# A token's place in the expert lists: two products over 24 and 16 columns in place of five over eight

## The chip, the cores and the metric

The kernel runs on one core of a Trainium2 chip. The core has four engines that compute and that run side by side, each with its own queue in order: TensorE (PE in the profile; its weight loads have a row of their own, PEld), VectorE (DVE), ScalarE (ACT) and GpSimd (POOL). SyncE (SP) issues transfers. The metric is the device time of one execution in microseconds (us), as the median of several runs.

## The reference

The inputs are `x` (4 x 512 tokens of 256), a context `ctx_1024` (4 x 1024 x 256), a mask and weights. The computation has two parts.

1. Cross attention with 16 heads of 16: `x = x + attention(layernorm(x), ctx, mask)`.
2. A block over the batch (the four entries of the first axis attend to each other, 16 query heads and 4 key heads), and then a mixture of experts: layer norm, a router over 8 experts, the two best experts for each token, for each of them `gelu(x w1) w2`, weighted by the router's probabilities:

```python
logits = einsum('th,eh->te', x, router_weight)
top_probs, top_idx = top_k(softmax(logits), 2)
h_mid = gelu(einsum('th,ehf->etf', x, moe_w1))
expert_out = einsum('etf,efh->eth', h_mid, moe_w2)
```

All is in float32.

## The kernel before

**Experts by lists.** A token's row is computed only by its two experts. For that, each expert has a list in a table in DRAM (2048 places for each expert), and each token's row is scattered to its place in two lists. Later the lists are read back in tiles of 128 rows, and each tile goes through one expert (`expert_x`, `expert_up`, `expert_down`). There are 39 such tiles. They are taken in lists that become known one after another: "a" (9 tiles), "b" (8), and "c" with "d" (22), whose places are only known when the last tokens have been routed.

**A half.** The second block works on halves: batch b and 256 of its 512 tokens, two tiles of 128, so there are eight halves (b, h). The generator `half(b, h)` holds the work of one in some 21 pieces, and each `yield` ends a piece. Behind the router (psl) it computes the softmax, the best expert and the second best, as zeros and ones over 8 experts in `picks[:, 0]` and `picks[:, 1]` (128 tokens in partitions x 2 tiles x 8). `chosen` is their sum: two tiles of 128 x 8 with a one where a token goes to that expert.

**The place.** A token's place in an expert's list is the list's length so far (`base`), plus the number of tokens before it in its own tile that go to that expert, plus, for the second tile, all of the first tile. TensorE counts that: with `before`, a 128 x 128 triangle of ones, and `ones`, 128 x 128 of ones. In the bank `psr` columns 0:8 get `before` x first tile, columns 8:16 get `before` x second tile + `ones` x first tile, and columns 16:24 get `ones` x both tiles, which is what is added to `base`. These are five products (L622 to L627). VectorE reads them (`place` L630, the new `base` L636), multiplies by `picks`, sums (`pos` L641) and makes whole numbers (`index` L643). GpSimd scatters the rows by `index` with four indirect DMAs (L653).

**What orders the work.** The order on every engine is written out by the program (`manual_schedule`): an engine takes its instructions as the Python code emits them.

- In the attention stage the code goes through 139 steps (10 of them ahead). A step has the maxima products (psm L1147, four), the score products (pss L1168, four), the exponentials on ScalarE, the maxima on VectorE (mx L1154), and the products with the values (av L1186). Other work is put behind a step by a planner, `Plan`: each piece has a cost on TensorE, a cost on VectorE, and a first and a last step. `spread` puts pieces into steps in order of their last step, by a rate, and with at most 2.0 of VectorE's cost in a step where a piece may still wait; `level` then moves pieces to where a step's modelled length grows least. The costs of the pieces of a half stand in `PARTS` as (TensorE, lag in steps, VectorE). The piece that picks the second expert has (0, 1, 1.6), the piece with the five products (1.1, 1, 1). Halves (0,0), (0,1), (1,0), (1,1) and the larger part of (2,0) and some of (2,1) are placed so.
- In the expert stage the code emits tile after tile and keeps a modelled clock for each engine (`clock`, `passed`). The rest of the halves (2,1), (3,0) and (3,1) is emitted between the tiles' pieces when the modelled clock of TensorE reaches the time due. The strings of the `yield`s are these costs: `"P1.1 D1"` says that the piece takes 1.1 on TensorE and then 1 on VectorE.

The pool `k2` gives each name two buffers, so `chosen` has two.

Of the kernel before, what the change touches and what calls it, by code (L numbers as in the profile page):

```python
# [7 lines left out]
F32 = mybir.dt.float32  # L8
I32 = mybir.dt.int32
AF = mybir.ActivationFunctionType  # L10
ALU = mybir.AluOpType
# [4 lines left out]
P = 128  # L16
B, S, SK, D = 4, 512, 1024, 256
H, DK, KVH, REP = 16, 16, 4, 4
E, F = 8, 512
# [154 lines left out]
def kernel(  # L174
# [21 lines left out]
    nc = tc.nc  # L196
# [3 lines left out]
    k2 = ctx.enter_context(tc.tile_pool(name="k2", bufs=2))  # L200
# [7 lines left out]
    def bank(name, maxima=False):  # L208
        if ahead[0] and not maxima:
            return pss.tile([P, 512], F32, tag="s", name=name)  # L210
        return psw.tile([P, 512], F32, tag="w", name=name)
# [202 lines left out]
    def half(b, h):  # L414


        n = f"{b}_{h}"
# [27 lines left out]
        for i in range(2):  # L445
            ps = bank(f"psq{n}_{i}")
            for c in range(KC):
# [4 lines left out]
                    start=(c == 0),  # L452
                    stop=(c == KC - 1),
# [85 lines left out]
        for i in range(2):  # L539
            ps = bank(f"psp{n}_{i}")  # L540
            for c in range(KC):
# [4 lines left out]
                    start=(c == 0),  # L546
                    stop=(c == KC - 1),
# [23 lines left out]
        ps = bank(f"psl{n}")  # L571
        for i in range(2):
            for c in range(KC):
# [4 lines left out]
                    start=(c == 0),  # L578
                    stop=(c == KC - 1),
                )  # L580
        small = [P, 2, E]
# [17 lines left out]
        def largest(dst, src, k):  # L599

            g = gate[:, b, t0 : t0 + 2, k : k + 1]
            nc.vector.tensor_reduce(gate[:, b, t0 : t0 + 2, k], src, AX.X, ALU.max)
            nc.vector.tensor_tensor(cand, src, g.to_broadcast(small), ALU.is_equal)
            nc.vector.tensor_tensor(cand, cand, ranks, ALU.mult)
            nc.vector.tensor_reduce(m, cand, AX.X, ALU.max)
            nc.vector.tensor_tensor(dst, cand, m.to_broadcast(small), ALU.is_equal)
# [2 lines left out]
        yield "D1.7"  # L609
        nc.vector.scalar_tensor_tensor(left, picks[:, 0], -2.0, lg, ALU.mult, ALU.add)  # L610
        largest(picks[:, 1], left, 1)
        chosen = k2.tile(small, F32, tag="chosen", name=f"chosen{n}")
        nc.vector.tensor_tensor(chosen, picks[:, 0], picks[:, 1], ALU.add)
        nc.gpsimd.tensor_copy(rows[:, :, D : D + E], picks[:, 0])
        token = named["token"]
        nc.gpsimd.tensor_copy(rows[:, :, D + E], token[:, NQT * b + t0 : NQT * b + t0 + 2])
# [2 lines left out]

        base, before, ones = named["base"], named["before"], named["ones"]  # L620
        ps = bank(f"psr{n}")
        nc.tensor.matmul(ps[:, 0:E], before, chosen[:, 0, :], start=True, stop=True)  # L622
        nc.tensor.matmul(ps[:, E : 2 * E], before, chosen[:, 1, :], start=True, stop=False)
        nc.tensor.matmul(ps[:, E : 2 * E], ones, chosen[:, 0, :], start=False, stop=True)
        for i in range(2):
            nc.tensor.matmul(
                ps[:, 2 * E : 3 * E], ones, chosen[:, i, :], start=(i == 0), stop=(i == 1)  # L627
            )
        place = k2.tile(small, F32, tag="place", name=f"place{n}")
        nc.vector.tensor_tensor(  # L630
            place,
# [9 lines left out]
        nc.vector.tensor_reduce(pos, picks, AX.X, ALU.add)  # L641
        index = k2.tile([P, 2, 2], I32, tag="index", name=f"index{n}")
        nc.vector.tensor_copy(index, pos)  # L643
        yield "P1.1 D1"
        for i in range(2):
            for k in range(2):
                scatter(index[:, k, i : i + 1], rows[:, i, :], scattered, "rows")
# [4 lines left out]
    def scatter(index, rows, group, name):  # L652
# [13 lines left out]
    PARTS = [  # L666
        (0, 1, 1.7), (0, 2, 1.9), (0.45, 1, 0), (1.3, 1, 0.4), (1.3, 1, 0.4), (0, 1, 0), (0, 2, 1.8),
        (0, 1, 0.8), (0, 1, 0), (0.45, 2, 0), (0.86, 1, 0.5), (0.86, 1, 0.5), (0, 1, 1.4),
        (0, 2, 1.3), (0.45, 1, 0), (0.9, 1, 0.4), (0, 1, 1.7), (0, 1, 1.6), (1.1, 1, 1), (0, 1, 0),
        (0, 1, 0),  # L670
    ]

# [212 lines left out]
    def project_o(b, t):  # L885
# [9 lines left out]
        nc.vector.tensor_tensor(xt[:, b, t, :], ps[:, 0:D], xt[:, b, t, :], ALU.add)  # L895

    halves = {(b, h): half(b, h) for b in range(B) for h in range(2)}

    with ExitStack() as actx:
# [67 lines left out]
        ps = bank("psmask")  # L967
# [8 lines left out]
        ps = bank("psfac")  # L976
# [242 lines left out]
        for b in range(B):  # L1219
            first = 32 * b - 32  # L1220
            if b:
                turned, projected = [], []
                for kc in range(NKC):
                    p = plan.add(
                        0.86,
                        first + (6 if kc > 3 else 1),
                        first + 4 + 11 * kc // 5,
                        project_k,
                        b,
                        kc,  # L1230
                        behind=projected[-1] if kc else None,
                        also=turned[kc - KRING] if kc >= KRING else None,
# [17 lines left out]
                for h in range(2):  # L1250
                    p = plan.add(0, first + 1, first + 3 + 3 * h, statistics_x, b, h, vector=1.4)
                    p = plan.add(
                        0,
                        first + 4,
                        first + 10 + 3 * h,
                        normalize_x,
                        b,
                        h,
                        behind=p,
                        lag=2,  # L1260
# [11 lines left out]
            for kc in range(NKC):  # L1272
                start = 32 * b - 10 + kc if kc >= 4 else kc if b == 1 else 32 * b - 34 + kc
                start = max(start, START + 1)
# [10 lines left out]
            p = divided[b * NC + NC - 1]  # L1285
            q = p
            for t in range(NQT):
                p = plan.add(
                    0.86, 32 * b + 34, 32 * b + 38 + t // 2, project_o, b, t, behind=q, vector=0.4
                )  # L1290
            for h in range(2):
                start = 32 * b + (40 if b < 2 else 38) + 4 * h
# [7 lines left out]
                p = None  # L1300
# [20 lines left out]
        p = lists_due  # L1321
        for n in range(3):
            p = plan.add(0, START, END - 10, next, first_list, None, behind=p, vector=1.8)
        p = plan.add(0, 8 * M - 8, END - 2, load_list, "a", FIRST, rows_a, behind=p)
# [51 lines left out]
        for T in range(START, END):  # L1376
            ahead[0] = T < 0
            n, kc = divmod(T, 8)
# [47 lines left out]
    start = late["start"] = epool.tile([P, 2 * E], F32, name="start")  # L1426
# [176 lines left out]
    n = 0  # L1603
    while going or n < len(tiles) + 2:
        if n < len(tiles) or not going:
            for behind, piece, args, work in PIECES:
# [5 lines left out]
                name, i = tiles[k][0:2]  # L1612
# [101 lines left out]
```

## Time and profile before

| | |
|---|---|
| median of 3 runs | 836.48 us (836.19 to 838.76) |
| profiled execution: its own time | 840.55 us |
| its span, first to last instruction | 838.8 us |
| TensorE busy | 791.9 us (94%) |
| VectorE busy | 561.7 us (67%) |
| ScalarE busy | 441.9 us (53%) |
| GpSimd busy | 290.0 us (35%) |
| mean granted TensorE clock | 0.985 |

The last score product of the attention stage ends at 634.1 us, the last product with the values at 637.3 us; the expert stage fills the rest. The five products run eight times:

| half | VectorE's `chosen` (L613) at | first product (L622) at |
|---|---|---|
| (0,0) | 351.57 | 354.97 |
| (0,1) | 372.20 | 373.84 |
| (1,0) | 526.49 | 529.04 |
| (1,1) | 544.89 | 550.20 |
| (2,0) | 630.83 | 631.72 |
| (2,1) | 643.85 | 647.20 |
| (3,0) | 712.32 | 714.37 |
| (3,1) | 722.07 | 723.72 |

A float32 product has two records for its two passes, so the five products of a half are ten records on TensorE and ten weight loads. A row of a timeline gives the start, the length from the first to the last of its records, the engine, the line, the operation, what is written and read, the shape and the number of records; in brackets stands the idle time of the engine before it and what ended it.

### The profile page before, as it was taken

Reading aid. Unit: us, or ns where it says so; the run is one execution under the profiler, and the core shown is the slowest. Engines: PE = TensorE matmul, PEld = TensorE weight load, DVE = VectorE, ACT = ScalarE, POOL = GpSimd, SP = SyncE. Lnnn points to the kernel's source line nnn. Section 1 sums busy time; section 2 is a strip of 40 time slices with the busy share of each in tenths; the row PEclk is TensorE's granted clock in tenths of the full one; section 3 lists DMA queues with packets and bytes.
Section 4 is the critical chain, followed back from the end, with each engine's and each line's share of the span. In section 5 each row is a group of like instructions: output and inputs, shape, how many; then the busy total and the mean of one; then the engine's idle time right before and its main releaser. Section 6 shows DMA issues by size and latency. Waiting matters only on the chain.

```text
span 838.8 us, 14851 instructions
## 1 busy us (share of the span) xinstructions
PE 791.9 (94%) x5255; PEld 409.2 (49%) x5255; DVE 561.7 (67%) x1335; ACT 441.9 (53%) x896; POOL 290.0 (35%) x445
## 2 busy tenths in 40 slices
PE   5999999999999999999999999999989989789993
PEld 4553433333433333444433333433326878789992
DVE  5687667666778777887786878888845587501033
ACT  2326666655565656555655565555555665434441
POOL 6815351001353300154653201223223564525531
PEclk9999999999999999999999999999989999989997
DMA  7229203408000000000000006000071450278954
GB/s 234 60 92 312 63 1 109 126 1 233 2 26 1 1 1 2 1 27 27 2 1 1 1 1 202 27 20 8 1 254 58 141 190 20 78 241 268 342 175 152
DMA packets 55641, 73.36 MB, mean 87 GB/s; under 512 B 5721, under 2 KB 40569, under 8 KB 55568
## 3 DMA queue, kind: packets, MB, share of 16 engines
q1 hardware_dynamic: 49968, 61.08, 23.8%
q0 software_dynamic: 4080, 10.07, 3.3%
q10 hardware_dynamic: 1520, 1.27, 0.5%
q8 instruction: 42, 0.69, 0.3%
q14 instruction: 31, 0.25, 0.1%
HBM read 42.88 MB, written 30.75 MB: 88 GB/s over the span
## 4 chain that ended last, share of the span: by engine, by line
PE 69%; DVE 11%; issue 10%; POOL 7%; DMA 1%; ACT 1%; POOLq 0%; ACTq 0%; SPq 0%; DVEq 0%
PE psm L1147 29%; PE av L1186 13%; PE psv L1061 4%; POOL given_rows L1483 4%; PE psk L1028 3%; DVE mx L1154 3%; PE pss L1168 3%; PE psq L448 2%; PE psp L542 2%; PE psy L1469 2%; PE psqt L1127 2%; PE pskt L1049 2%; PE psp L888 2%; PE psu L1451 2%; PE psq L1107 1%
## 5 line engine op out<-in xcount | busy, mean ns | idle before, releaser
L1154 DVE TENSOR_REDUCE mx<-psm 128x1 f32<-128x512 f32 x512 | 326.1, 683 | 115.2 <-PE pss L1168 100.7
L1176 ACT ACTIVATE ex<-pss 128x512 f32<-128x512 f32 x512 | 277.4, 596 | 203.6 <-PE pss L1168 192.4
L1147 PE MATMUL psm<-kT_odd,shared 32*128 32x512 f32 x512 | 152.1, 639 | 3.1 <-ACT shared L1135 2.1
L1168 PE MATMUL pss<-qt,shared 32*128 32x512 f32 x512 | 151.6, 639 | 0.0
L1168 PE MATMUL pss<-qt,kT_odd 32*128 32x512 f32 x512 | 146.5, 646 | 0.9 <-ACT ex L1176 0.9
L1147 PE MATMUL psm<-shared 32*128 32x512 f32 x512 | 143.0, 639 | 0.7 <-ACT shared L1135 0.7
L1186 PE MATMUL av<-ex,vaug 128*32 128x512 f32 (+1 forms) x888 | 107.1, 551 | 4.4 <-DVE sm L274 4.1
L1451 PE MATMUL psu<-shared 128*128 128x128 f32 x624 | 78.2, 277 | 2.9 <-ACT shared L1436 2.4
L993 POOL TENSOR_TENSOR shared<-shared 128x256 f32<-128x256 f32 x44 | 33.5, 761 | 135.0 <-ACT shared L1036 113.6
L1147 PEld LDWEIGHTS psm<-kT_odd,shared 32*128 32x128 f32 x512 | 43.8, 183 | 74.3 <-DVE mx L1154 33.8
L1451 PEld LDWEIGHTS psu<-shared 128*128 128x128 f32 x624 | 76.6, 193 | 6.9 <-ACT shared L1436 4.0
L1469 PE MATMUL psy<-shared 128*128 x312 | 77.6, 393 | 1.1 <-issue 0.6
L1147 PEld LDWEIGHTS psm<-shared 32*128 32x128 f32 x512 | 42.3, 183 | 65.5 <-DVE mx L1154 29.2
L1469 PEld LDWEIGHTS psy<-shared 128*128 128x128 f32 x312 | 58.0, 196 | 9.4 <-issue 1.7
L1186 PEld LDWEIGHTS av<-ex,vaug 128*32 128x32 f32 x888 | 17.8, 108 | 89.2 <-issue 81.2
L1460 ACT ACTIVATE shared<-psu 128x512 f32<-128x512 f32 x39 | 23.4, 599 | 49.2 <-PE psu L1451 22.7
L1168 PEld LDWEIGHTS pss<-qt,kT_odd 32*128 32x128 f32 x512 | 42.8, 184 | 8.3 <-ACT ex L1176 3.8
L995 POOL TENSOR_TENSOR shared<-shared 128x128 f32<-128x128 f32 x88 | 44.8, 530 | 0.0
L1168 PEld LDWEIGHTS pss<-qt,shared 32*128 32x128 f32 x512 | 43.6, 183 | 2.0 <-ACT ex L1176 1.5
L268 POOL TENSOR_TENSOR rm<-vm,power 128x2 f32<-128x2 f32 x8 | 5.7, 712 | 109.4 <-DVE vm L555 87.0
L653 POOL DMA_INDIRECT table<-rows,index x32 | 32.4, 1013 | 31.9 <-issue 11.4
L1515 DVE SCALAR_TENSOR_TENSOR y<-y,gate,xt 128x256 f32<-128x256 f32 x16 | 7.7, 481 | 45.9 <-DMA y<-given_rows 45.9
(296 smaller groups left out, 1041.4 us busy)
## 6 DMA issues: line engine op xcount, KB each, us to landing
shared<-in_moe_w_dram SPq DMA_DIRECT2D x47, 512.0 KB
table<-zeros SPq DMA_DIRECT2D x8, 2120.0 KB
shared<-in_ctxT_dram SPq DMA_DIRECT2D x8, 512.0 KB
y<-given_rows SPq DMA_DIRECT2D x12, 256.0 KB
shared<-table SPq DMA_DIRECT2D x18, 132.5 KB
xt<-in_x_dram SPq DMA_DIRECT2D x4, 512.0 KB
rows_d<-table SPq DMA_DIRECT2D x13, 132.5 KB
out_dram<-y SPq DMA_DIRECT2D x6, 256.0 KB
```

The source lines that it names most:

```text
L653: inst = nc.gpsimd.indirect_dma_start(out=table, out_offset=bass.IndirectOffsetOnAxis(ap=index, axis=0), in_=rows, in_offset=None, bounds_ ...
L993: engine.tensor_tensor(a, src, over(f[:, 0:DK]), ALU.mult)
L995: engine.tensor_tensor(r[:, :, i::2], src[:, :, 1 - i :: 2], over(f[:, DK + i : 2 * DK : 2]), ALU.mult,)
L1061: nc.tensor.matmul(ps[:, 0:D], context(b, kc, c), wv_sb[:, c, :], start=(c == 0), stop=(c == KC - 1),)
L1147: nc.tensor.matmul(ps, q1[m][rows, t * P : (t + 1) * P], kT[b % 2][rows, g, h * 512 : (h + 1) * 512], start=True, stop=True,)
L1154: nc.vector.tensor_reduce(mx[m][:, t, j, h : h + 1], ps, AX.X, ALU.max)
L1168: nc.tensor.matmul(ps, kT[b % 2][rows, g, kc * P : (kc + 1) * P], q2[m][rows, :], start=True, stop=True,)
L1176: nc.scalar.activation(ex[m, kc, j], ps, AF.Exp, scale=SCALE)
L1186: nc.tensor.matmul(av[m][32 * j : 32 * j + 32, over], vaug[(b * NKC + kc) % VRING][:, 4 * g + j, :], x[:, over], start=(kc == 0), stop=(kc ...
L1451: nc.tensor.matmul(ps_of[k][:, of], w1_of[k][:, c, of], xT_of[k][:, c, :], start=(c == 0), stop=(c == KC - 1),)
L1469: nc.tensor.matmul(ps_of[k], h_of[k][:, f * P : (f + 1) * P], w2_sb[:, bass.ds(weights_of[k] + f * D, D)], start=(f == 0), stop=(f == F // ...
L1483: inst = nc.gpsimd.indirect_dma_start(out=given_rows[n], out_offset=bass.IndirectOffsetOnAxis(ap=number[name][:, i, :], axis=0), in_=y, in ...
```

## The change

`chosen` becomes a part of a tile `marks` of 128 x 5 x 8 with one buffer: rows 0 and 1 are the two tiles as before, row 2 is zero, row 3 is a copy of row 0, and row 4 is the sum of rows 0 and 1. So `before` times rows 0 to 2 (24 columns) and `ones` times rows 3 and 4 (16 columns, added to columns 8:24) give the same 24 columns in the bank. GpSimd writes the zeros, VectorE the copy and the sum, in the piece that picks the second expert. That piece's cost for VectorE in the plan goes from 1.6 to 1.8; that of the products on TensorE from 1.1 to 0.45, in `PARTS` and in the `yield`.

```diff
         largest(picks[:, 1], left, 1)
-        chosen = k2.tile(small, F32, tag="chosen", name=f"chosen{n}")
+
+        marks = k2.tile([P, 5, E], F32, tag="marks", name=f"marks{n}", bufs=1)
+        chosen = marks[:, 0:2, :]
+        nc.gpsimd.memset(marks[:, 2, :], 0.0)
         nc.vector.tensor_tensor(chosen, picks[:, 0], picks[:, 1], ALU.add)
+        nc.vector.tensor_copy(marks[:, 3, :], marks[:, 0, :])
+        nc.vector.tensor_tensor(marks[:, 4, :], marks[:, 0, :], marks[:, 1, :], ALU.add)
         nc.gpsimd.tensor_copy(rows[:, :, D : D + E], picks[:, 0])
...
         ps = bank(f"psr{n}")
-        nc.tensor.matmul(ps[:, 0:E], before, chosen[:, 0, :], start=True, stop=True)
-        nc.tensor.matmul(ps[:, E : 2 * E], before, chosen[:, 1, :], start=True, stop=False)
-        nc.tensor.matmul(ps[:, E : 2 * E], ones, chosen[:, 0, :], start=False, stop=True)
-        for i in range(2):
-            nc.tensor.matmul(
-                ps[:, 2 * E : 3 * E], ones, chosen[:, i, :], start=(i == 0), stop=(i == 1)
-            )
+        flat_marks = marks.rearrange("p i e -> p (i e)")
+        nc.tensor.matmul(ps[:, 0 : 3 * E], before, flat_marks[:, 0 : 3 * E], start=True, stop=False)
+        nc.tensor.matmul(
+            ps[:, E : 3 * E], ones, flat_marks[:, 3 * E : 5 * E], start=False, stop=True
+        )
...
-        yield "P1.1 D1"
+        yield "P0.45 D1"
...
     PARTS = [
         (0, 1, 1.7), (0, 2, 1.9), (0.45, 1, 0), (1.3, 1, 0.4), (1.3, 1, 0.4), (0, 1, 0), (0, 2, 1.8),
         (0, 1, 0.8), (0, 1, 0), (0.45, 2, 0), (0.86, 1, 0.5), (0.86, 1, 0.5), (0, 1, 1.4),
-        (0, 2, 1.3), (0.45, 1, 0), (0.9, 1, 0.4), (0, 1, 1.7), (0, 1, 1.6), (1.1, 1, 1), (0, 1, 0),
+        (0, 2, 1.3), (0.45, 1, 0), (0.9, 1, 0.4), (0, 1, 1.7), (0, 1, 1.8), (0.45, 1, 1), (0, 1, 0),
         (0, 1, 0),
     ]
```

## The prediction, written before the result was known

> **What bounds the kernel now.** I read the page's busy times and its chain first, then the rows of the products' bank (psr), then the timeline of TensorE around them, then the busy times of single steps, and last the timelines of GpSimd and TensorE at the end of the routing.
>
> ```profile
> PE 791.9 (94%) x5255; PEld 409.2 (49%) x5255; DVE 561.7 (67%) x1335; ACT 441.9 (53%) x896; POOL 290.0 (35%) x445
> ...
> PE 69%; DVE 11%; issue 10%; POOL 7%; DMA 1%; ACT 1%; POOLq 0%; ACTq 0%; SPq 0%; DVEq 0%
> ```
>
> TensorE is busy for 94% of the span and carries 69% of the chain: what leaves its queue leaves the time, unless another engine is close behind it just there. So the price of the five products comes first. TensorE's timeline at half (0,0), and one row from the expert stage for scale:
>
> ```profile
> 354.97 0.39 PE L622 MATMUL psr<-chosen,before 128*128 128x8 f32 x2
> 355.21 0.37 PE L623 MATMUL psr<-chosen,before 128*128 128x8 f32 x2
> 355.43 0.37 PE L624 MATMUL psr<-chosen,ones 128*128 128x8 f32 x2
> 355.66 0.59 PE L626 MATMUL psr<-chosen,ones 128*128 128x8 f32 x4
> 356.10 0.63 PE L294 MATMUL psx<-ident,rows 128*128 128x128 f32 x4
> ```
>
> ```profile
> 718.28 1.95 PE L1451 MATMUL psu<-shared 128*128 128x128 f32 x16
> ```
>
> From start to start a product takes 0.22 to 0.24 us, and from the first to what follows the five take 1.13. The psu row holds eight products over 128 columns, and the next row on TensorE starts at 720.06: 1.78 / 8 = 0.2225 each. So 8 columns and 128 columns cost the same, and 24 and 16 lie between: 0.22 each, bounded from both sides.
>
> How close VectorE is, by the busy times of the stretches in which halves (0,0), (0,1), (1,0), (1,1) and (2,0) have their products. The columns: stretch, length, busy time and instructions of PE, PEld, DVE, ACT and POOL, the granted clock, DMA.
>
> ```profile
> 351.83:356.67 4.84, 4.84 (x40) 2.32 (x39) 3.93 (x11) 2.54 (x5) 0.00 (x0) 1.00 0.00 0
> 370.63:375.06 4.43, 4.42 (x37) 1.97 (x36) 4.20 (x12) 2.71 (x5) 0.87 (x4) 1.00 0.00 0
> 524.81:530.16 5.35, 5.35 (x45) 2.97 (x44) 4.93 (x15) 3.29 (x7) 0.00 (x0) 1.00 0.00 0
> 534.30:551.42 17.12, 16.95 (x132) 6.69 (x131) 16.25 (x51) 10.50 (x21) 5.37 (x7) 1.00 0.09 33
> 629.65:632.93 3.28, 3.28 (x27) 1.66 (x26) 1.35 (x2) 3.10 (x7) 1.38 (x3) 1.00 0.02 9
> ```
>
> The reader is to see that TensorE fills every one of them, that VectorE has 0.91, 0.23, 0.42, 0.87 (over four steps) and 1.93 us free, and that less than 0.67 free means less than a full gain.
>
> The expert stage, at half (3,1): GpSimd's timeline, then TensorE's restart.
>
> ```profile
> 722.35 0.98 POOL L1483 DMA_INDIRECT given_rows<-shared,numberb  x1 [0.30 <-issue]
> 723.31 0.23 POOL L614 COPY rows<-picks 128x16 f32<-128x16 f32 x1
> ...
> 725.15 0.98 POOL L1483 DMA_INDIRECT given_rows<-shared,numberb  x1 [1.50 <-DVE place L630]
> 726.62 0.97 POOL L653 DMA_INDIRECT table<-rows,index  x1 [0.48 <-issue]
> ```
>
> ```profile
> 736.18 0.66 PE L1433 MATMUL psxe<-ident,shared 128*128 128x128 f32 x2 [6.56 <-DMA shared<-table]
> ```
>
> TensorE has run out of tiles of list b and stands 6.56 us until list c is read, behind the last scatter. From 740 to 820 it is full without a gap. So in this stage not TensorE's sum counts but how early the scatter of half (3,1) starts.
>
> **The change, part by part.**
>
> *TensorE.* Three products go: 3 x 0.2225 = 0.67 us in each half, 5.34 over eight. That is the most the change can save directly.
>
> *VectorE.* A copy and a sum of 128 x 8 come, in the piece before. The nearest rows are a copy of 128 x 8 (L1536, 0.163) and a sum of 128 x 8 (L755, 0.166). In the picking chain each operation that needs the one before starts 0.205 behind it, and one that doesn't starts 0.09 behind (`chosen` at 544.89, the next maximum at 544.98). So they cost 0.30 (one waits) to 0.41 (both). I take 0.41, since both read what was just written.
>
> *GpSimd.* A memset of 128 x 8: between L263 (128 x 1, 0.098) and L962 (128 x 16, 0.125), 0.11. It stands ahead of the copy L614. In all eight halves L614 started before the products, by 0.41 us at the least (half (3,1), 723.31 against 723.72) and 1.0 at the next (half (2,0), 630.71 against 631.72). TensorE now waits for it too; what stands behind that wait is the whole of TensorE's queue. That cover of 0.3 after the memset hides it; without it, each 0.1 is 0.1 on the path, and if the next `given_rows` (725.15 to 726.13) came ahead of it, some 2.4. The single buffer of `marks` makes the memset wait for the products of the half before; they lie 8 us back at the closest (714.4 to 715.6 against 723.3), so it costs nothing.
>
> *The five halves of the attention stage.* The products give 0.67, less what VectorE can't follow.
> - (0,0): 0.91 free in the step, so 0.67.
> - (0,1): 0.23 free, but the next steps have room, and the plan sees a step with 0.65 less in it and may put other work there: 0.5, between 0.23 and 0.67.
> - (1,0): 0.42 free, and the added 0.41 fall into a step with 0.26 free (3.94 busy of 4.20 from 520.61): 0.4.
> - (1,1): VectorE has no gap over 0.06 us in the four steps before, so the added 0.41 count, and then 0.67 goes: 0.2, between a loss of 0.41 and a gain of 0.67.
> - (2,0): VectorE is free, and `chosen` is done at 631.05, at 631.46 with the additions, before 631.72: 0.6.
>
> Sum 2.4; the ends are 1.1 (0.67 + 0.23 + 0 - 0.41 + 0.6) and 3.3.
>
> *The three halves of the expert stage.* VectorE waits 0.59, 3.09 and 2.70 us for psr there, so its additions are covered by TensorE's pieces ahead of the products (without that, 0.41 each). Half (2,1): the statistics of half (3,0) stand on VectorE right behind `index` (649.22): 0.6. Half (3,0): 0.67 sooner, and with it its four scatters and the `given_rows` behind them. Half (3,1): `index` comes 2 x 0.67 = 1.34 sooner, but the scatter stands behind the `given_rows` of 725.15, which itself moves by 0.67 and ends at 725.46; 0.30 later is 725.76, against 726.62: 0.86 for both. Sum 1.5; the ends are 0.5 (only one of the three arrives) and 2.0.
>
> *The plan and the clock.* Every cost that changes can move pieces. Moved work costs the same on TensorE; what could cost is a piece of VectorE or GpSimd that falls in front of TensorE. I take 0; the trace bounds it by its own worst, the wait of `av` at 614.09 for VectorE, 4.1 us, as a loss, and by as much of a gain where the order now meets it. In the expert stage the modelled clock falls by 0.65 where the real one does by 0.67, so I expect the order to keep step.
>
> Together 2.4 + 1.5 = 3.9 us. Against the profiled execution: 840.55 - 3.9 = 836.65 (span 838.8 to 834.9). That execution lies 4.07 over the median of the runs; against the median 836.48 - 3.9 = 832.6.
>
> *A rule against it.* Two operations of VectorE in these very lists took far longer than their like:
>
> ```profile
> 629.67 1.12 DVE L606 TENSOR_TENSOR picks<-cand,m 128x16 f32<-128x16 f32 x1
> 630.83 0.22 DVE L613 TENSOR_TENSOR chosen<-picks 128x16 f32<-128x16 f32 x1
> ```
>
> The others of L606 take 0.17; GpSimd's L557 ran from 629.50 to 630.77. The Trainium skill, page SBUF — State Buffer, section "Who interferes with whom", says that a VectorE operation with two inputs in SBUF contends with a GpSimd operation that reads SBUF, that a copy can contend too, and that the loser waits for the whole of the other. By it each added operation may be held by GpSimd's copies beside it, 0.2 each (L614, L616), at halves (0,1) and (2,0): an estimate of 833.0 in place of 832.6.
>
> **The rivals.**
> 1. *VectorE takes over in the five attention halves*: no gain there and 0.41 lost each: 836.48 - 1.5 + 2.05 = 837.0. For it: 16.25 busy of 17.12 at half (1,1). Against it: at (0,0) and (2,0) it has 0.9 and 1.9 free.
> 2. *The new order eats it*: a wait of the size of 614.09's, 4.1, comes from moved pieces: 832.6 + 4.1 = 836.7. For it: five costs change in a greedy plan. Against it: from 500 us on the pieces have hardly a step of room to move in.
> 3. *Slower*: the additions are held by GpSimd, as at 629.67 (1.12 - 0.17 = 0.95), in each attention half, where VectorE then bounds: 5 x (0.41 + 0.95) = 6.8 lost, 1.5 won: 836.48 + 5.3 = 841.8. It ends over before as soon as the five lose 0.3 each on the mean. For it: the rows above. Against it: 2 of 16 operations nearby were held, and GpSimd has 0.2-us copies at that place.
> 4. *It doesn't do what it says*: wider products cost more. The psu row leaves no room for that; no chance is given.
>
> **How the numbers follow.** Forecast 0.6, rival 1 0.15, rival 2 0.15, rival 3 0.1. About 0.3% (2.5 us) is what can be told from no change here. The forecast's own range is 1.6 to 5.3 saved (its two sums' ends), 831.2 to 834.9, and most of it lies below 834.0; with rivals 1 and 2 inside 0.3% for the most part: faster 0.57, same 0.31, slower 0.12. The range goes from 830.3 (the full 5.34 and some luck in the order) to 837.8, past rivals 1 and 2.
>
> **What would show it.** After: psr with four records a half, 0.45 us; the step of half (0,0) 0.67 shorter; no wait of TensorE for GpSimd ahead of psr; the last `av` ending 2.4 us earlier; the first scatter of (3,1) 3.9 earlier, the wait for list c about as long. It would be wrong if the attention stage ended no earlier (rivals 1, 2: look for VectorE ahead of psm, or a new long wait of `av`), or if the restart of list c moved less than the stage before it.

## The result and the profile after

The changed kernel takes 845.50 us (median of three runs, 844.44 to 846.73), against 836.48 before: a ratio of 1.0102, 95% interval 1.0081 to 1.0123. It is slower by about 9 us, where 3.9 less had been forecast. The profiled execution spans 845.0 us, 6.2 more than before.

The busy times and the engines of the chain, from the page of the changed kernel:

```profile
PE 787.7 (93%) x5199; PEld 403.8 (48%) x5199; DVE 564.9 (67%) x1351; ACT 441.7 (52%) x896; POOL 290.2 (34%) x453
...
PE 62%; DVE 13%; issue 11%; POOL 9%; DMA 2%; ACT 2%; POOLq 0%; SPq 0%; ACTq 0%; DVEq 0%
```

TensorE has 4.2 us less to do, near the 5.3 of the forecast, and carries 62% of the chain instead of 69%. It is idle for longer, and VectorE, GpSimd and the DMAs stand in the chain in its place. So the work went and waits came.

TensorE's timeline of the changed kernel, at halves (1,0) and (1,1):

```profile
524.82 0.66 PE L1130 MATMUL psqt<-ident,shared 128*128 128x128 f32 x4 [1.49 <-DVE shared L1161]
...
552.25 0.66 PE L294 MATMUL psh<-ident,hn 128*128 128x128 f32 x4 [1.52 <-DVE mx L1157]
552.94 0.37 PE L628 MATMUL psr<-marks,before 128*128 128x24 f32 x2
553.15 0.37 PE L629 MATMUL psr<-marks,ones 128*128 128x16 f32 x2
```

The two products are there, four records. In the eight halves they start 0.14 to 0.25 us apart, and the next product follows 0.36 to 0.55 behind the first of them, where with five it followed 1.03 to 1.21 behind. Two waits of 1.5 us for VectorE are new; before, TensorE had no gap there. The last `av` ends at 640.32 (before 637.31), 3.0 us later. Not all of that is the change's: 1.3 us stand there at the first maxima product already (29.83 against 28.53), and 1.6 come from a stretch at 554 us in which TensorE is granted about half its clock (last section).

The expert stage takes 204.7 us (before 201.5). GpSimd's timeline of the changed kernel, at halves (3,0) and (3,1):

```profile
722.38 0.10 POOL L615 MEMSET marks<- 128x8 f32 x1 [1.05 <-PE psr L629]
...
724.44 0.99 POOL L656 DMA_INDIRECT table<-rows,index  x1 [1.69 <-DVE index L646]
725.73 0.98 POOL L656 DMA_INDIRECT table<-rows,index  x1 [0.30 <-issue]
727.01 0.97 POOL L1486 DMA_INDIRECT given_rows<-shared,numberb  x1 [0.30 <-DVE base L639]
728.29 0.97 POOL L656 DMA_INDIRECT table<-rows,index  x1 [0.30 <-issue]
...
737.54 0.97 POOL L656 DMA_INDIRECT table<-rows,index  x1 [0.30 <-issue]
```

Before, the scatters came in two trains, those of half (3,0) from 717.26 and those of (3,1) from 726.62:

```profile
717.26 0.97 POOL L653 DMA_INDIRECT table<-rows,index  x1 [3.10 <-DVE lg L586]
...
721.08 0.97 POOL L653 DMA_INDIRECT table<-rows,index  x1 [0.30 <-issue]
...
730.75 0.97 POOL L653 DMA_INDIRECT table<-rows,index  x1 [0.30 <-issue]
```

Now all eight stand in one train, with three result transfers (L1486) between them, each 1.27 to 1.57 us behind the one ahead. The products of (3,0) and (3,1) begin at 721.74 and 726.08, 4.3 us apart where it was 9.4: (3,0) has become 7.4 later, and the two halves run side by side. The last scatter begins at 737.54 (before 730.75), and TensorE restarts with list c later, by its timeline in the changed kernel:

```profile
742.50 0.69 PE L1436 MATMUL psxe<-ident,shared 128*128 128x128 f32 x2 [8.39 <-DMA shared<-table]
```

What follows the restart takes as long as before (102.5 us against 102.7). So in this execution the last `av` came 3.0 us later, and 3.3 more were lost between it and 742.5. The diff changes two things: the operations, and three costs in the tables that order the work.

### The profile page after: what moved, and what is told of

Its sections match the earlier page's. It is cut to its first block, busy times and chain, and to the rows that moved or that the text cites. A ratio compares the mean times of both kernels' runs of the same rounds, so it can differ in the third digit from the quotient of the medians.

```text
span 845.0 us, 14764 instructions
## 1 busy us (share of the span) xinstructions
PE 787.7 (93%) x5199; PEld 403.8 (48%) x5199; DVE 564.9 (67%) x1351; ACT 441.7 (52%) x896; POOL 290.2 (34%) x453
## 3 DMA queue, kind: packets, MB, share of 16 engines
q10 hardware_dynamic: 1520, 1.27, 0.5%
## 4 chain that ended last, share of the span: by engine, by line
PE 62%; DVE 13%; issue 11%; POOL 9%; DMA 2%; ACT 2%; POOLq 0%; SPq 0%; ACTq 0%; DVEq 0%
PE psm L1150 27%; PE av L1189 13%; PE psv L1064 3%; DVE mx L1157 3%; POOL given_rows L1486 3%; PE pss L1171 3%; PE psk L1031 3%; PE psq L448 2%; PE psqt L1130 2%; PE psu L1454 2%; PE pskt L1052 1%; PE psp L542 1%; PE psq L1110 1%; POOL shared L998 1%; PE psp L891 1%
## 5 line engine op out<-in xcount | busy, mean ns | idle before, releaser
L1179 ACT ACTIVATE ex<-pss 128x512 f32<-128x512 f32 x512 | 277.5, 596 | 205.7 <-PE pss L1171 198.1
L1454 PE MATMUL psu<-shared 128*128 128x128 f32 x624 | 79.9, 280 | 3.1 <-ACT shared L1439 3.0
L656 POOL DMA_INDIRECT table<-rows,index x32 | 32.5, 1015 | 25.6 <-issue 10.3
```

Source lines behind the costliest of these rows:

```text
L656: inst = nc.gpsimd.indirect_dma_start(out=table, out_offset=bass.IndirectOffsetOnAxis(ap=index, axis=0), in_=rows, in_offset=None, bounds_ ...
L1179: nc.scalar.activation(ex[m, kc, j], ps, AF.Exp, scale=SCALE)
L1454: nc.tensor.matmul(ps_of[k][:, of], w1_of[k][:, c, of], xT_of[k][:, c, :], start=(c == 0), stop=(c == KC - 1),)
```

## The experiments

Theory A: the order is to blame, through the new costs. Rival B: the new operations are. Rival C: the smaller cost makes the modelled clock run ahead, in proportion. Ratios are to the kernel before, run beside each on the same chip. Positions come from one profiled execution, and single executions differ: those of the kernel before took 834.5 to 842.0 us. What is worth a few us is therefore read from the ratios.

| kernel | median us | before | ratio (95%) | last `av` ends | from there to the end |
|---|---|---|---|---|---|
| before | 836.48 | | | 637.31 | 201.5 |
| change | 845.50 | 836.48 | 1.0102 (1.0081 to 1.0123) | 640.32 | 204.7 |
| operations, old costs | 836.15 | 838.71 | 0.9971 (0.9958 to 0.9984) | 636.37 | 198.0 |
| change, old clock cost | 837.79 | 838.71 | 0.9993 (0.9976 to 1.0009) | 638.90 | 198.8 |
| change, old plan costs | 846.52 | 838.71 | 1.0084 (1.0056 to 1.0111) | 637.21 | 208.3 |
| five products, new costs | 851.39 | 838.71 | 1.0144 (1.0124 to 1.0165) | 642.50 | 210.4 |
| old plan, clock cost 0.5 | 836.24 | 837.69 | 0.9986 (0.9973 to 1.0000) | 636.25 | 197.2 |
| additions on GpSimd | 833.85 | 837.69 | 0.9952 (0.9937 to 0.9968) | 638.17 | 195.8 |
| three products, no additions | 834.60 | 837.69 | 0.9967 (0.9954 to 0.9980) | 636.83 | 197.8 |
| additions only | 838.85 | 837.69 | 1.0015 (1.0004 to 1.0026) | 637.73 | 198.1 |
| change, due time 1.05 | 837.84 | 838.69 | 0.9988 (0.9974 to 1.0003) | 639.22 | 199.4 |
| before, due time 1.15 | 843.68 | 838.69 | 1.0054 (1.0036 to 1.0072) | 638.71 | 205.6 |
| additions on GpSimd, due time 0.9 | 835.46 | 838.69 | 0.9952 (0.9935 to 0.9969) | 636.98 | 197.4 |
| operations, VectorE's plan cost 1.8 | 833.93 | 837.34 | 0.9950 (0.9932 to 0.9968) | 636.99 | 195.7 |

### The operations without their costs

```diff
-        yield "P0.45 D1"
+        yield "P1.1 D1"
...
-    ... (0, 1, 1.8), (0.45, 1, 1), ...
+    ... (0, 1, 1.6), (1.1, 1, 1), ...
```

> The two products and the marks as in the change, but the old costs in PARTS (1.6 and 1.1) and the old P1.1 in the yield, so that every engine's order is that of before. Theory A (the new costs move pieces, and the moved pieces make the loss; the products themselves save what was forecast): 836.5 - 3.9 = 832.6, between 831.2 and 834.9; the attention stage ends 1.1 to 3.3 sooner than before, list c starts sooner too. Theory B (the operations themselves make it: VectorE's additions, GpSimd's memset ahead of TensorE, the single buffer): near the changed kernel, 843 to 846.

0.9971: faster by 2.4 us, not by the 3.9 of the forecast. By the profiles every engine has its instructions in the order of before, and with that the loss is gone. B falls as the cause of the 9 us.

### Either cost alone, and both without the operations

The old cost in the `yield` only:

```diff
-        yield "P0.45 D1"
+        yield "P1.1 D1"
```

> The change with the old P1.1 in the yield: only the planner of the attention stage sees the new costs. Theory A: the attention stage ends 3.0 later than before, as in the changed kernel (its steps 519.99 to 526.28 and 547.27 to 560.29 keep their waits), the expert stage is 1.5 shorter than before: 836.5 + 3.0 - 1.5 = 838.0. Theory B: 843 to 846.

The old costs in `PARTS` only:

```diff
-    ... (0, 1, 1.8), (0.45, 1, 1), ...
+    ... (0, 1, 1.6), (1.1, 1, 1), ...
```

> The change with the old costs in PARTS: only the modelled clock of the expert stage sees the new cost. Theory A: the attention stage ends 2.4 sooner than before, the expert stage is 3.2 longer, as in the changed kernel (wait for list c 8 us and more in place of 6.6): 836.5 - 2.4 + 3.2 = 837.3. Theory B: 843 to 846.

The kernel before, its five products untouched, with all the new costs:

```diff
-        yield "P1.1 D1"
+        yield "P0.45 D1"
...
-    ... (0, 1, 1.6), (1.1, 1, 1), ...
+    ... (0, 1, 1.8), (0.45, 1, 1), ...
```

> The kernel before with its five products and without the marks, but with the new costs in PARTS and in the yield. Theory A: the changed kernel's order with dearer products, 845.5 plus up to 3.9: 845 to 849. Theory B: the costs alone do little: 835 to 838.

The new plan costs 1.6 us (medians 837.79 against 836.15, 0.9993 against 0.9971). The last `av` comes 2.5 later, but 0.95 of that stands there at the second step, long before the plan moves anything. Where: above all at half (1,0). Its products go one step later, and a projection (psp) and a transposition (psqt) into the step at 520, which takes 6.3 us in place of 4.4; the three steps there take 15.5 in place of 13.9. That is the wait of 1.49 in the changed kernel. Two steps at half (1,1) grow from 10.2 to 11.4; elsewhere steps grow and shrink. The new cost in the `yield` costs the expert stage 10.3 us (208.3 against 198.0), and 1.0084 against 0.9971. That is three times what A had expected, and the time lies near where B had expected it; what speaks against B are the operations without the new costs, and the costs without the operations. The costs alone, with no operation changed, lose 12.7 us, more than A allowed. So A holds, and the larger part is the modelled clock's.

### Is the clock's loss in proportion?

```diff
-        yield "P1.1 D1"
+        yield "P0.5 D1"
```

(from the kernel with the old costs)

> The change with the old costs in PARTS and P0.5 in the yield: 0.05 more than the 0.45 of the change. Theory A (a due time that falls just behind the modelled clock: half (3,0)'s piece with hn is due at 18.65 where the clock stands at 18.60 with 0.45; with 0.5 both stand at 18.65, and the piece is not put behind one more tile piece): like the run with all the old costs, 2 to 3 us under before, first products of (3,0) some 74 us behind the last av. Theory C (the lower clock costs in proportion to 0.65): hardly better than the run with 0.45, 844 to 846.

At 0.5 the time is near that of 1.1, 0.9986 (0.9971 there, the intervals overlap); at 0.45 it was 1.0084. Nothing in proportion: C falls, and there is an edge between 0.5 and 0.45. Following the modelled clock through the code, with the plan of before, shows it. The piece that normalizes `hn` of half (3,0) (its `yield "D1.1!"`, L424) is due at 19.250, and at cost 1.1 TensorE's modelled clock stands at exactly 19.250 when it is asked: the piece is emitted. At 0.45 the clock stands 0.65 lower, at 18.600. The due time goes down by 0.60 only, to 18.650, because VectorE's modelled clock was not waiting for TensorE the whole time. The piece is 0.05 short of its due time, another part of a tile goes first, and it is emitted at 19.500, with that of half (3,1) behind it at 19.750. Before, the two were emitted at 19.250 and 20.400. Further on the products of (3,0) and (3,1) are emitted at 68.20 and 72.25 of the modelled clock, where it was 67.60 and 76.50: the halves stand side by side in the written order already. Two runs test that reading.

The whole change, with that due time 0.05 sooner. The line is run for half (3,1) too, so its piece moves along; with (3,0)'s alone moved, the code writes the same order:

```diff
-            yield "D1.1!"
+            yield "D1.05!"
```

> The whole change, its costs included, with one figure altered: the due time of the piece that normalizes half (3,0)'s hn is 1.05 steps instead of 1.1. Nothing else differs. Theory A (the loss of the expert stage is a near miss in the planner: the new cost 0.45 takes 0.65 from TensorE's modelled clock but only 0.60 from the due time of that piece, so that it is 0.05 not yet due, goes behind another tile of list b, and halves (3,0) and (3,1) then run side by side): the order of the expert stage is again that of the kernel with the old clock; psr of (3,0) and of (3,1) lie 8 to 9 us apart, the scatters come in two trains, the expert stage falls from 204.7 to about 199, and the time from 845.5 to 837 to 839 (ratio 0.997 to 1.003). Rival B (the smaller clock costs in proportion, all over the stage, or the products and additions themselves do): a due time 0.05 earlier changes next to nothing, 844 to 847 (ratio 1.008 to 1.012).

The kernel before, with it 0.05 later (with (3,0)'s alone moved, the order differs by one swap of neighbours):

```diff
-            yield "D1.1!"
+            yield "D1.15!"
```

> The kernel before, with its five products and all its costs, and the one due time of half (3,0)'s hn piece put from 1.1 to 1.15 steps: nothing of the change is in it. Theory A (near miss in the planner): this alone makes halves (3,0) and (3,1) run side by side, the eight scatters stand in one train, the expert stage takes 207 to 211 in place of 201.5 and the time is 842 to 847 (ratio 1.006 to 1.012). Rival B (the loss needs something that the change brings: its smaller clock, its additions, its single buffer of marks): as before, ratio 0.998 to 1.002.

The first runs at 0.9988: the expert stage takes 199.4 us, and all its loss is gone with one figure. The second takes 1.0054 (expected 1.006 to 1.012: a little less, same sign), with nothing of the change in it. GpSimd's scatters in the kernel before with 1.15:

```profile
725.87 0.98 POOL L653 DMA_INDIRECT table<-rows,index  x1 [2.97 <-issue]
...
728.44 0.97 POOL L1483 DMA_INDIRECT given_rows<-shared,numberb  x1 [0.30 <-DVE place L630]
...
739.05 0.97 POOL L653 DMA_INDIRECT table<-rows,index  x1 [0.30 <-issue]
```

and in the whole change with 1.05:

```profile
716.04 0.98 POOL L656 DMA_INDIRECT table<-rows,index  x1 [2.42 <-DVE lg L586]
...
719.89 0.97 POOL L656 DMA_INDIRECT table<-rows,index  x1 [0.30 <-issue]
...
725.62 0.97 POOL L656 DMA_INDIRECT table<-rows,index  x1 [0.86 <-issue]
...
729.75 0.97 POOL L656 DMA_INDIRECT table<-rows,index  x1 [0.30 <-issue]
```

One train from 725.9 to 740.0 in the first, with one gap of 1.85 us; two in the second, with the last scatter over at 730.7. So the kernel before gets the train of the changed kernel without any of its operations.

### Which of the plan's costs

From the kernel with the old costs:

```diff
-    ... (0, 1, 1.6), (1.1, 1, 1), ...
+    ... (0, 1, 1.8), (1.1, 1, 1), ...
```

> The kernel with the change's operations and the old costs, but with VectorE's new cost of the picking piece in the plan (1.8 in place of 1.6); TensorE's 1.1 for the products stays in both places. With both new costs in the plan the last product with the values ended at 638.90, with both old ones at 636.37. Theory A1 (TensorE's 0.45 is the cost that moves the products of half (1,0) and what stands around them, and that loses the 2.5 us): with 1.8 alone some pieces of the second quarter of the attention stage trade places, the products of half (1,0) stay in their step, the last product with the values ends at 636.0 to 637.0 and the time is 834 to 837 (ratio 0.995 to 0.999 to the kernel before). Rival A2 (VectorE's 1.8 does it): 638.0 to 639.5, and 836.5 to 839 (ratio 0.998 to 1.001).

636.99 and 0.9950. So VectorE's 1.8 does no harm, and it is TensorE's truer cost, 0.45 for 1.1, that makes the plan worse. The 0.45 was not run with the old 1.6, and by which of its comparisons the plan then moves half (1,0)'s products was not followed.

### Why the products are worth less than 2.4 us in the attention stage

With the order held, the steps of the kernel with the old costs can be laid beside those of before (length of the step with the products, and of its neighbours that changed by over 0.1 us):

| half | forecast | before | old costs | gained | with the additions on GpSimd |
|---|---|---|---|---|---|
| (0,0) | 0.67 | 4.84 + 5.09 | 4.17 + 5.48 | 0.28 | 0.28 |
| (0,1) | 0.5 | 4.43 + 5.50 | 3.69 + 5.77 | 0.47 | 0.38 |
| (1,0) | 0.4 | 4.20 + 5.35 + 4.14 | 4.44 + 4.86 + 4.63 | -0.24 | 0.01 |
| (1,1) | 0.2 | 5.34 + 4.62 | 5.03 + 5.20 | -0.27 | 0.01 |
| (2,0) | 0.6 | 3.28 | 2.62 | 0.66 | 0.66 |
| sum | 2.4 | | | 0.90 | 1.34 |

In two other executions of the same attention stage (old plan, clock costs 0.45 and 0.5) the step of (0,1) takes 4.08 and 4.07 in place of 3.69, which leaves a gain of 0.09 there and a sum of 0.5; the other halves repeat within 0.02.

In the step of the products the gain is there, 0.31 to 0.74 in the table. But in the first four halves the steps beside it give a part or all of it back. The busy times of the next step of half (0,0), first before and then with the old costs (stretch, length, PE, PEld, DVE, ACT, POOL, granted clock, DMA):

```profile
356.67:361.76 5.09, 5.09 (x38) 2.35 (x37) 4.71 (x15) 3.19 (x6) 2.46 (x3) 1.00 0.06 22
```

```profile
356.51:361.99 5.48, 5.48 (x39) 2.64 (x38) 5.24 (x18) 3.32 (x7) 2.22 (x3) 1.00 0.01 5
```

VectorE had 0.38 us free there before. The step ahead is 0.67 shorter, so 0.5 of VectorE's work slides into this one, and it has 0.24 left. That this makes the step longer is read from these busy times and not shown by a wait. Half (1,0) shows what TensorE then waits for. VectorE's copy of the queries, ahead of the place, before and with the old costs:

```profile
529.31 0.68 DVE L1133 COPY qt<-psqt 128x512 f32<-128x512 f32 x1
```

```profile
529.52 0.68 DVE L1136 COPY qt<-psqt 128x512 f32<-128x512 f32 x1
```

TensorE's first score products of the step behind the places, before and with the old costs:

```profile
530.16 0.69 PE L1168 MATMUL pss<-qt,kT_odd 32*128 32x512 f32 x1
530.18 0.69 PE L1168 MATMUL pss<-qt,kT_odd 32*128 32x512 f32 x1
```

```profile
529.70 0.69 PE L1171 MATMUL pss<-qt,kT_odd 32*128 32x512 f32 x1
530.22 0.69 PE L1171 MATMUL pss<-qt,kT_odd 32*128 32x512 f32 x1
```

The products end 0.46 sooner, but the second group starts at 530.2 in both. Before, `qt` was ready at 529.99, while the five products ran. Now it is ready at 530.20, as the second group starts: the products had covered VectorE, and the additions have made it 0.2 later. That the one waits for the other is read from the times; the profile names no releaser there.

Three runs set the additions apart from that. On GpSimd:

```diff
-        nc.vector.tensor_copy(marks[:, 3, :], marks[:, 0, :])
-        nc.vector.tensor_tensor(marks[:, 4, :], marks[:, 0, :], marks[:, 1, :], ALU.add)
+        nc.gpsimd.tensor_copy(marks[:, 3, :], marks[:, 0, :])
+        nc.gpsimd.tensor_tensor(marks[:, 4, :], marks[:, 0, :], marks[:, 1, :], ALU.add)
```

(old costs)

> All the old costs, and the copy and the sum for rows 3 and 4 of marks are made by GpSimd in place of VectorE. Theory D (VectorE's additions take back the attention stage's gain in the step behind each products' step): the steps after 66, 70, 103 and 108 give back 0.3 less each, the attention stage ends 1.2 to 1.5 sooner than with the additions on VectorE, time 1.2 to 1.5 under that run. Theory E (VectorE bounds there without them too): no sooner, within 0.4.

No additions at all, the second tile's counts by a product of `ones` with row 0 twice and the total by one more, with the zeros written once:

```diff
-        nc.gpsimd.memset(marks[:, 2, :], 0.0)
-        nc.vector.tensor_copy(marks[:, 3, :], marks[:, 0, :])
-        nc.vector.tensor_tensor(marks[:, 4, :], marks[:, 0, :], marks[:, 1, :], ALU.add)
...
-            ps[:, E : 3 * E], ones, flat_marks[:, 3 * E : 5 * E], start=False, stop=True
+            ps[:, E : 3 * E].rearrange("p (i e) -> p i e", e=E),
+            ones,
+            marks[:, 0, :].unsqueeze(1).to_broadcast(small),
+            start=False,
+            stop=False,
...
+        nc.tensor.matmul(ps[:, 2 * E : 3 * E], ones, marks[:, 1, :], start=False, stop=True)
```

(old costs)

> All the old costs; three products (before over the two tiles and a row of zeros that is written once for all halves; ones over the first tile twice, read with a repeating pattern; ones over the second tile), so VectorE and GpSimd do in a half what they did before. TensorE saves 2 x 0.2225 = 0.445 a half. Theory D: it keeps it all in the attention stage: 5 x 0.445 = 2.2 there and 1.0 behind it, 3.2 under before. Theory E: it gives most of it back in the attention stage, 1.3 under before.

The memset and the additions with the five products kept, and nobody reading rows 2 to 4:

```diff
-        nc.tensor.matmul(ps[:, 0 : 3 * E], before, flat_marks[:, 0 : 3 * E], start=True, stop=False)
-        nc.tensor.matmul(
-            ps[:, E : 3 * E], ones, flat_marks[:, 3 * E : 5 * E], start=False, stop=True
-        )
+        nc.tensor.matmul(ps[:, 0:E], before, chosen[:, 0, :], start=True, stop=True)
...
```

(old costs)

> The five products of before and all the old costs, but the marks are written (memset on GpSimd, copy and sum on VectorE), and rows 2 to 4 are read by nobody. Theory D: the additions alone cost 0.3 at each of the five attention halves, up to 1.5 over before, nothing behind it. Theory E: they fit into VectorE's free time, within 0.4 of before.

The additions alone make four steps longer, by 0.30, 0.24, 0.18 and 0.29 us, 1.0 in all, at halves (0,1), (1,0) and (1,1): 1.0015. Taken off VectorE they give 0.9952. With three products and no additions, 0.9967. The intervals of both overlap with the 0.9971 above, so the steps must decide.

In both kernels without additions on VectorE halves (1,0) and (1,1) come out even (0.00 to 0.02): something else bounds the steps there, by their busy times VectorE's other work, and the additions only turn that zero into a loss of a quarter of a microsecond each. So D holds at these two halves alone, and was too simple. With the additions on GpSimd the steps give 0.44 more than with them on VectorE, not 1.2 to 1.5. That execution's last `av` is even 1.8 later; 1.3 of it falls on a stretch at about half the granted clock, from 579 to 583 us. With three products the steps give 1.1, not 2.2. Its median lies 3.1 under before, near D's 3.2; but the steps and the 1.0 behind them make 2.1, which is inside the interval too (1.7 to 3.9), so that nearness shows nothing.

### A version with distance from the edge

From the kernel with the additions on GpSimd:

```diff
-            yield "D1.1!"
+            yield "D0.9!"
```

> The best version so far (two products, old costs, the copy and the sum of marks on GpSimd) with the due time of half (3,0)'s hn piece at 0.9 steps instead of 1.1, well away from the tie; the order differs by a few pieces only. Theory A: the time stands where the kernel with 1.1 stood, 832.5 to 835 (ratio 0.994 to 0.997). Rival: the tie at 1.1 was also the best place for the piece, and putting it earlier delays the tiles of list b: 836 to 839 (ratio 0.998 to 1.002).

0.9952 again, so the tie is not needed for the gain. This version and the two others at 0.995 beat both kernels; their intervals don't tell the three apart.

## Why the prediction was wrong, step by step

- **The step that failed** is "the plan and the clock": "I take 0 ... I expect the order to keep step", since the modelled clock falls by 0.65 and the real one by 0.67. That the two agree says nothing of the order. What is compared is TensorE's modelled clock with a due time that comes from another engine's modelled clock, and that moved by 0.60. 0.05 of a modelled microsecond is worth 1.1% of the time (0.9988 against 1.0102, each to its own runs of before). The bound was wrong as well: 4.1 us either way, from the largest wait in the trace, where the plan costs 1.6 and the clock some 9 (1.0084 against 0.9971, 1.0102 against 0.9993). A wait in the trace doesn't bound what another order does.
- *TensorE*: right. Two products of 24 and 16 columns in place of five of 8 bring the next product 0.66 to 0.69 sooner in every half; 0.66 to 0.67 came off the step where VectorE is free.
- *VectorE's additions*, 0.30 to 0.41, 0.41 taken: in the changed kernel the copy starts 0.21 behind the sum that it needs, and the second sum 0.08 to 0.12 behind the copy, so about 0.29, the lower end. The 1.0 us that they cost alone over four steps fits.
- *GpSimd's memset*, nothing: right in length (0.09 to 0.14). That the single buffer costs nothing held for the old order only. With (3,0) and (3,1) side by side, the memset waits 1.05 us for the products of the half ahead, and VectorE's L616 waits 0.35.
- *Five attention halves*, 2.4 with an end at 1.1: measured 0.90, and 0.5 in two other executions, below the end. The working looked at VectorE's room in the step of the products and in those ahead, and for (0,1) took room behind it for granted. What was missing is the step behind: work that slides out of a shorter step must fit there.
- *Three expert halves*, 1.5: right within its ends. With the old costs the expert stage is 3.56 shorter, of which 1.69 is the granted clock (below): 1.87. The index of (3,1) starts 3.57 sooner against the last `av`, less 1.69: 1.88, forecast 0.6 + 1.34.
- *The sum*: 3.9, with the order held 2.8 by the span (4.5 less 1.69) and 2.4 by the medians (0.29% of 838.7; the interval is 1.3 to 3.5). So the operations are right in sign and over 1 us too large, because of the attention stage.
- *The rule on GpSimd and VectorE* (the Trainium skill, SBUF — State Buffer, "Who interferes with whom") and rival 3: no added operation waited for the whole of a GpSimd copy. The longest of the eight copies took 0.212 us (0.17 to 0.19 the others), of the eight sums 0.163, in the changed kernel.
- *Rival 1*, VectorE takes over: half true, at (1,0) and (1,1). *Rival 2*, the new order eats it: the right mechanism. It was given 0.15, and a price of 4.1 that couldn't reach past "no change"; it needed a price that ends slower. Three costs change, not five, and against it stood that the pieces have "hardly a step of room" from 500 us on: one step was enough at half (1,0).

## What to carry to other kernels

Where a program orders the work by costs, an edit of a cost is a change of the schedule: price it apart from the operations, by following which comparisons flip, and first run the operations with the old costs. A gain on one engine must be followed into the next step, where the runner-up's work slides. A due time that meets its clock exactly is an edge: 0.05 put the kernel before up by 0.5% and the changed one down by 1.1%.

## What was not expected of the hardware

TensorE's granted clock fell to about a half for some 3.5 us after a wait of 1.7 us in one execution and not in another. The busy times by stretches, before and with the old costs, at the same work (the granted clock is the third number from the end):

```profile
690.00:692.00 2.00, 2.00 (x7) 1.59 (x7) 1.93 (x4) 0.90 (x3) 1.21 (x1) 0.59 0.00 0
692.00:694.00 2.00, 2.00 (x7) 1.61 (x6) 0.82 (x1) 0.37 (x1) 1.84 (x3) 0.56 0.00 0
```

```profile
688.00:690.00 2.00, 2.00 (x10) 1.77 (x11) 1.90 (x5) 1.16 (x4) 0.99 (x1) 1.00 0.00 0
690.00:692.00 2.00, 2.00 (x13) 1.82 (x12) 1.75 (x3) 0.33 (x1) 1.96 (x2) 1.00 0.00 0
```

TensorE's timeline at the wait ahead of them, before and with the old costs:

```profile
688.91 0.66 PE L294 MATMUL psa<-ident,at 128*128 128x128 f32 x4 [1.71 <-DVE at L525]
...
689.74 3.22 PE L1469 MATMUL psy<-shared 128*128 x8
```

```profile
687.12 0.66 PE L294 MATMUL psa<-ident,at 128*128 128x128 f32 x4 [1.70 <-DVE at L525]
...
687.93 1.99 PE L1472 MATMUL psy<-shared 128*128 x8
```

The same eight products take 3.22 and 1.99 us behind waits of 1.71 and 1.70. With the psp behind them it is 5.24 and 3.55 to the next product, a difference of 1.69 us. The changed kernel shows a clock of 0.54 to 0.60 from 554 to 558, behind the wait of 1.52 at 552.25; the change with the old clock cost, with the same order there, waits 1.27 at that place, keeps 1.00, and is 1.64 us faster over that step. The Trainium skill (TensorE: Matmul & The Clock Gate, "Part 1: The HAM clock gate") has the half clock come after at least one idle window of about 3.4 us. Here 1.5 to 1.7 us were followed by it, and not each time; what decides is open. For the reading of single profiles it means that a gap of that size can make one execution 1.6 to 1.7 us longer than another of the same order, so the split of 3.0 and 3.3 us given above is one execution's.
